# A GRU over 128 steps on one core: two more steps' inputs loaded ahead of r's last input weight, their reset products moved to the start, z's biases spread in another PSUM bank

## The chip, the cores and the metric

The kernel runs on one core of a Trainium2 chip. Its time is the device time of one execution in microseconds (us). The kernel before takes 1255.2 us, the median of three runs (1254.98 to 1255.48). A separate execution was profiled; durations below come from it.

## The reference

A batch of B = 64 sequences of T = 128 steps and width D = 512 goes through a GRU (gated recurrent unit) with state width 512, all in float32, and the result is added to the input:

```
for t in 0 .. 127:
    z = sigmoid([x_t, h] @ Wz + bz)          # Wz, Wr, Wh: 1024 x 512
    r = sigmoid([x_t, h] @ Wr + br)
    c = tanh([x_t, r * h] @ Wh + bh)
    h_new = (1 - z) * h + z * c
    h = tanh(h_new @ Wp + bp) if t % 4 == 3 and t < 127 else h_new
    out[:, t] = x_t + h_new
```

The first 512 rows of each weight meet x (here called the input weights, tile `wx`), the last 512 meet the state (`wh`). The input products do not depend on the state and may be computed ahead of the step that needs them; the state products may not.

## The kernel before, in words

The batch is cut into two halves of 32 (h = 0, 1) that run through the recurrence a little apart, so that one half's elementwise work lies under the other's products. A product of one step, one gate and one k (a quarter of the inner dimension, K = 4) is a *unit* (L246, called through `product` and `plain_unit`): four instructions of 128 x 32 by 128 x 256, eight records in the trace (each float32 product shows as two).

From group 2 on (a group is four steps) the input products are made by a scheme that shares products between steps. The first four steps, group 0, are done plainly: `plain(t, gates)` gives their units. Steps 0 and 1 are made ahead of the recurrence. Some units of steps 2 and 3 also stand ahead of it, the others are put in a queue from which the recurrence fills its gaps (`fill`, with the number of units per place in `HEAD`, `PLACES` and `TAIL`).

The order of the instructions on each engine is the order in which the Python code issues them (the pool is in manual schedule); only the waits are derived from what is read and written. What matters here is the start:

- **SP's DMA queue.** Rows of step 0 (L141; step 1's go through ACT's queue), r's input weight in three pieces (k = 0, k = 1, k = 2 and 3; `load_wx`, L127), z's and h's input weight in two pieces each, then step 2's x (`load_step(2)`, four transfers of 32 KB, L122), the state weight of r (L108), step 3's x (`load_step(3)`), the state weights of z and h, and the later loads. Each transfer of SP uses one of eight semaphores in turn, so it is issued when the transfer eight places before it (ACT's L141 among them) has landed. All of SP's transfers go to the same DMA queue.
- **GpSimd (POOL)** issues the biases' loads (L145), then copies one element of r's third piece (L154). Because of that copy it issues the initial state's rows (L156) only when the piece has landed. After VectorE's `sum_outer_1` it makes sums of weights.
- **TensorE (PE).** 28 products with zeros (`idle`), the transposes of steps 0 and 1 (`turn_rows`, L306), four more with zeros; r's units of steps 0 and 1 for k 0, for k 1, for k 2 and 3, as the pieces land; z's units of steps 0 and 1 in two halves, with the bias spreads between them; h's units of steps 0 and 1; then `both(8)`, eight units of step 2 (r and z); then step 0 of the recurrence, from `rec<-wh,hT_init`.
- **The biases.** `split_bias` (L205 to L210, VectorE) cuts them into three bfloat16 parts. `spread` (L217) multiplies these by a picking matrix into a PSUM bank, and ACT copies the result to `bias_x` (L226). r's and h's go to `scratch_y`, z's to the second half of `scratch_a`. `add_bias` (L483, VectorE) adds a bias to finished units and writes `cp`, from which ACT seeds the accumulators (`seed`, L442).
- **VectorE (DVE)** in order: copies of the turned rows (L311), `split_bias`, inner sums of input weights for r and z (L362 to L365, twice four), `add_bias` of r for steps 0 and 1, the first inner sum for h, `join_x(0, 2)` (L297, turns step 2's x into `xT`, the products' left side), the second inner sum for h, `sum_outer_1` (L354), the turn of the initial state (`hT_init`, L284), `add_bias` of z, `join_x(0, 3)`, `add_bias` of h and of step 2's r and z.

PSUM banks are named `scratch_q, r, a, x, y`. Step 0 has r in q's first half, step 1 in a's; step 2 has r in q's first and z in its second half, step 3 the same in a (`banks`). A unit that is first to write a bank is marked so (`start`); a gate that comes second in its bank is not marked (`second` in `plain_unit`).

Of the kernel before, what the change touches and what calls it, by code (L numbers as in the profile page):

```python
# [18 lines left out]
def kernel(  # L19
# [18 lines left out]
    S = 2  # L38
# [57 lines left out]
    def part(q):  # L96
        return slice(q * V, (q + 1) * V)
# [20 lines left out]
        xr[g] = xrp.tile([P, Q4, S, J], F32, tag="xr", name=f"xr_{g}")  # L118

    def load_step(t):  # L120
        for q in (0, 2, 1, 3):
            nc.sync.dma_start(  # L122
                out=xr[0][part(q), t], in_=x[:, t, ts(q, J)].rearrange("(h b) u -> b h u", h=S)
            )

    def load_wx(i, k0, k1):
        nc.sync.dma_start(  # L127
            out=wx[:, k0:k1, i, :],
            in_=gates_in[i][:D].rearrange("(p k) n -> p k n", k=K)[:, k0:k1],
        )  # L130
# [8 lines left out]
    )  # L139
    for t in range(2):  # L140
        both_queues[t].dma_start(out=x_rows[:, ts(t, D)], in_=x[:, t, :])  # L141
    for k0, k1 in ((0, 1), (1, 2), (2, K)):
        load_wx(R, k0, k1)
    for i, b in enumerate((br, bh, bz)):
        nc.gpsimd.dma_start(out=bias_in[:, i, :], in_=b.rearrange("(q j) -> q j", q=NQ))  # L145
    dummy = const.tile([1, 1], F32, name="dummy")
# [2 lines left out]
    for i in (Z, H_):  # L149
        for k in (0, 2):  # L150
            load_wx(i, k, k + 2)
    load_step(2)
    held = const.tile([1, 1], F32, name="held")
    nc.gpsimd.tensor_copy(held, wx[0:1, 3, R, 0:1])  # L154
    for h in range(S):
# [47 lines left out]
    def split_bias():  # L203
        high, low = thirds[:NQ], thirds[2 * V : 2 * V + NQ]
        nc.vector.tensor_copy(high, bias_in)  # L205
        nc.vector.tensor_sub(rest, bias_in, high)
        nc.vector.tensor_copy(middle, rest)
        nc.vector.tensor_copy(thirds[V : V + NQ], middle)
        nc.vector.tensor_sub(rest, rest, middle)
        nc.vector.tensor_copy(low, rest)  # L210
# [80 lines left out]
    def join_x(g, i):  # L291
        if g * Q4 >= T:
            return
        if g not in xT:
            xT[g] = xtp.tile([P, Q4, C, P], F32, tag="xT", name=f"xT_{g}")
        src = xr[g] if g < FIRST else xs[g]
        nc.vector.transpose(  # L297
            out=xT[g][:, i].rearrange("p c (a h b) -> p h (c a) b", a=S, h=S),
            in_=src[:, i].rearrange("p h (e k) -> p h k e", k=K),
        )  # L300
# [173 lines left out]
    def banks(t):  # L474
        first, second = scratch[:2] if t % 2 == 0 else scratch[2:4]
        if t < 2:
            return first[:, : S * J], second[:, : S * J], scratch[4][:, ts(t, S * J)]
        return first[:, : S * J], first[:, S * J :], second[:, : S * J]

    def add_bias(t, gates):  # L480
        new_cp(t // 2)
        for i in gates:
            nc.vector.tensor_add(  # L483
                G[t][:, :, :, i, :],
                banks(t)[i].rearrange("p (h c n) -> p c h n", h=S, c=C),
                bias_x[:, :, :, i, :],
            )

    def plain_unit(t, e, k, start, end=None, gates=()):
        g, i = divmod(t, Q4)  # L490
        bank = (q_bank, q_bank, r_bank) if t % 2 == 0 else (a_bank, a_bank, x_banks[0])
        second = H_ if t == 1 else None if t == 0 else Z
        return (
            lambda h: product(
                banks(t)[e], h, xT[g][:, i], wx[:, :, e, :], k, start and e != second
            ),
            S * J,
            {bank[e]},
            end,
            {bank[e] for e in gates},  # L500
        )

    def plain(t, gates=(R, Z, H_)):
        order = [(e, k) for e in gates for k in range(K)]
        if t == Q4 - 1:
            order = [(e, k) for k in range(K) for e in gates]
        return [
            plain_unit(
                t,
                e,  # L510
                k,
                k == 0,
                *((lambda: add_bias(t, gates), gates) if t > 1 and (e, k) == order[-1] else ()),
            )
            for e, k in order
        ]
# [254 lines left out]
    def both(n):  # L771
        for _ in range(n):
            for h in range(S):
                for _ in fill(1, h):
                    pass

    def now(units):
        put(units)
        both(len(units))

    first = {i: [plain(t, (i,)) for t in range(2)] for i in (R, Z, H_)}
    idle(28)
    turn_rows(0, scratch[4])
    turn_rows(1, scratch[3])
    split_bias()
    idle(4)
    for part_k in (slice(0, 1), slice(1, 2), slice(2, K)):
        for t in range(2):
            now(first[R][t][part_k])
    load_wh(R)  # L790
    load_step(3)
    load_wh(Z)
    load_wh(H_)
    later_loads()
    for t in range(2):
        now(first[Z][t][:2])
    spread(scratch[4], slice(0, 2), (R, H_))
    spread(scratch[2][:, S * J :], slice(2, 3), (Z,))
    for t in range(2):
        now(first[Z][t][2:])  # L800
    for i in (1, 2):
        sum_inner(i, nc.vector, slice(0, 2))
    for t in range(2):
# [1 line left out]
    for h in range(S):  # L805
        seed(R, 0, h)
    sum_inner(1, nc.vector, slice(2, 3))
    join_x(0, 2)
    sum_inner(2, nc.vector, slice(2, 3))
    sum_outer_1(nc.vector)  # L810
    hT = new_T("hT", "hT_init")
# [3 lines left out]
    for t in range(2):  # L815
        add_bias(t, (Z,))
    seed(Z, 0, 0)
    join_x(0, 3)
    for half_k in (slice(0, 2), slice(2, K)):
        for t in range(2):  # L820
            now(first[H_][t][half_k])
# [4 lines left out]
        sum_inner(i, nc.gpsimd)  # L826
    sum_outer(3)
    nc.gpsimd.tensor_sub(bias_d, bias_x[:, 1], bias0)
    put(plain(2, (R, Z)) + plain(3) + plain(2, (H_,)))
    both(8)  # L830

    state = {0: (h_init, hT)}

# [384 lines left out]
```

## Time and profile before

| | |
|---|---|
| median of the runs | 1255.2 us |
| profiled execution | 1255.74 us |
| its span, first to last instruction | 1253.6 us |
| TensorE granted clock | 1.000 |
| TensorE busy in 7.70 to 9.19 us | 0.21 us of 1.49 |
| TensorE busy in 9.19 to 33.5 us | all of it |
| DMA in 7.70 to 9.19 us | 363 GB/s, share 1.02 |
| start of the recurrence (first weight load of step 0) | 21.42 us |

Times in the trace are counted from the span's start. A row of the timeline has the start, the length of the whole group of instructions in us, the engine (PEld is TensorE's weight load, SPq the DMA-issuing queue of SP), the line, the operation, output <- input with its shape, and how many; in brackets stands the idle time before it and what ended that. A row of the waits has who waited for what, then the sum in us, the number of times and the longest. A row of DMA issues has how many, KB each and the us from issue to landing. A row of a DMA queue has its packets, MB, and the time that they took as a share of sixteen engines in the window.

### The profile page before, as it was taken

The page shows a single profiled execution, that of the slowest core. Times are in us where ns is not written, and L with a number is a line of the kernel's source. Part 1 is how long each engine was busy: PE and PEld are TensorE (multiplying, and loading weights), DVE is VectorE, ACT ScalarE, POOL GpSimd, SP SyncE. Part 2 cuts the span into 40 slices and gives each one's busy share as a digit, 9 for nine tenths or more (in the row PEclk, how much of TensorE's full clock was granted, in tenths as well). Part 3 has the DMA queues.
Part 4 walks back from the last instruction along what each step waited for, and adds up shares of the span by engine and source line. Part 5 has one row for each costly group of instructions (what it writes and reads, how often), then busy time and mean ns, then how long its engine had stood idle before and what let it go on. Part 6 is the DMA issues. An engine that isn't in the chain of part 4 may idle for free.

```text
span 1253.6 us, 61573 instructions
## 1 busy us (share of the span) xinstructions
PE 1246.9 (99%) x26384; PEld 1174.0 (94%) x26384; DVE 806.2 (64%) x2177; ACT 830.0 (66%) x2666; POOL 908.8 (72%) x1032
## 2 busy tenths in 40 slices
PE   9999999999999999999999999999999999999998
PEld 5899999999999999999999999999999999999987
DVE  5666666666666666666666666666666666666554
ACT  2566666766666676766666667666666666666664
POOL 4988777777876778767778677786777777777630
PEclk9999999999999999999999999999999999999999
DMA  8311212121111110221201211111111112111011
GB/s 257 83 31 42 53 37 53 36 54 39 35 53 49 41 49 24 53 53 37 54 24 49 53 41 50 36 43 47 53 38 39 49 39 53 39 52 27 12 39 35
DMA packets 112360, 61.14 MB, mean 49 GB/s; under 512 B 12844, under 2 KB 109368, under 8 KB 112088
## 3 DMA queue, kind: packets, MB, share of 16 engines
q1 hardware_dynamic: 111656, 56.90, 16.8%
q8 instruction: 208, 3.41, 1.2%
q14 instruction: 64, 0.52, 0.1%
q0 software_dynamic: 256, 0.14, 0.1%
q10 hardware_dynamic: 176, 0.16, 0.0%
HBM read 40.38 MB, written 16.78 MB: 46 GB/s over the span
## 4 chain that ended last, share of the span: by engine, by line
PE 99%; DMA 1%; SPq 0%; DVE 0%; issue 0%; ACT 0%
PE rec L246 44%; PE rec_z L246 16%; PE scratch_r L246 14%; PE scratch_q L246 11%; PE scratch_a L246 5%; PE scratch_y L246 4%; PE scratch_x L246 4%; DMA wx<-in_L_cond_Wr_dram 1%; PE scratch_a L541 0%; PE scratch_r L541 0%; PE scratch_q L541 0%; PE scratch_y L541 0%; PE scratch_x L541 0%; SPq L127 0%; SPq L141 0%
## 5 line engine op out<-in xcount | busy, mean ns | idle before, releaser
L246 PE MATMUL rec<-wh,rhT 128*32 128x256 f32 x4032 | 370.1, 379 | 0.0
L246 PE MATMUL rec<-wh,hT 128*32 128x256 f32 x3008 | 276.2, 379 | 0.0
L246 PE MATMUL rec_z<-wh,hT 128*32 128x256 f32 x3008 | 276.2, 379 | 0.0
L246 PEld LDWEIGHTS rec<-wh,rhT 128*32 128x32 f32 x4032 | 247.5, 110 | 16.7 <-ACT rec L442 0.3
L281 ACT ACTIVATE scratch_r<-rec 64x128 f32<-64x128 f32 x504 | 126.0, 250 | 129.9 <-PE rec L246 65.4
L442 ACT COPY rec<-cp 64x256 f32<-64x256 f32 x504 | 186.9, 371 | 19.4 <-DVE cp L483 0.2
L246 PEld LDWEIGHTS rec_z<-wh,hT 128*32 128x32 f32 x3008 | 190.5, 110 | 6.2
L246 PEld LDWEIGHTS rec<-wh,hT 128*32 128x32 f32 x3008 | 184.0, 110 | 11.2 <-ACT rec_z L442 0.4
L281 ACT ACTIVATE rec_z<-rec_z 64x128 f32<-64x128 f32 x488 | 122.0, 250 | 91.3 <-PE rec_z L246 79.7
L281 ACT ACTIVATE c<-rec 64x128 f32<-64x128 f32 x504 | 136.7, 271 | 61.5 <-PE rec L246 50.4
L968 POOL TENSOR_TENSOR xr<-xr,h 128x256 f32<-128x256 f32 x125 | 109.3, 874 | 85.8 <-DVE h L1138 71.9
L711 POOL TENSOR_TENSOR cp<-mb,mb 128x768 f32<-128x768 f32 x76 | 139.1, 1830 | 9.4 <-DVE mb L677 5.7
L711 POOL TENSOR_TENSOR mb<-mb,mb 128x768 f32<-128x768 f32 x58 | 106.3, 1832 | 45.8 <-DVE mb L677 45.8
L711 POOL TENSOR_TENSOR cp<-mb 128x768 f32<-128x768 f32 x46 | 84.3, 1832 | 56.8 <-ACT rec_z L442 55.4
L246 PE MATMUL scratch_r<-tw,s 128*32 128x192 f32 x928 | 120.9, 326 | 0.0
L650 ACT COPY cq<-scratch_q 128x384 f32<-128x384 f32 x212 | 102.1, 481 | 19.4 <-PE scratch_q L246 17.9
L667 DVE TENSOR_TENSOR cx<-scratch_r,cx 128x384 f32<-128x384 f32 x106 | 59.0, 557 | 84.5 <-PE scratch_r L246 69.0
L246 PE MATMUL scratch_q<-tt,s 128*32 128x192 f32 x928 | 103.6, 326 | 0.0
L1102 DVE SCALAR_TENSOR_TENSOR keep<-rec_z,h 128x256 f32<-128x256 f32 x91 | 38.6, 424 | 95.6 <-ACT rec_z L281 89.2
L673 DVE TENSOR_TENSOR mb<-scratch_q,cx 128x384 f32<-128x384 f32 x106 | 59.0, 557 | 62.5 <-ACT cq L650 62.5
L1081 DVE TENSOR_TENSOR rh<-scratch_r,h 128x128 f32<-128x128 f32 x188 | 54.8, 292 | 59.2 <-ACT scratch_r L281 59.2
L246 PE MATMUL rec<-wp,hT 128*32 128x256 f32 x992 | 91.4, 379 | 0.0
(250 smaller groups left out, 3899.9 us busy)
## 6 DMA issues: line engine op xcount, KB each, us to landing
out_dram<-xr SPq DMA_DIRECT2D x250, 64.0 KB, 1.8
xr<-in_x_dram SPq DMA_DIRECT2D x248, 64.0 KB, 2.1
xs<-in_x_dram SPq DMA_DIRECT2D x240, 64.0 KB, 2.1
wx<-in_L_cond_Wz_dram SPq DMA_DIRECT2D x2, 512.0 KB
wx<-in_L_cond_Wh_dram SPq DMA_DIRECT2D x2, 512.0 KB, 9.5
wh<-in_L_cond_Wr_dram SPq DMA_DIRECT2D x2, 512.0 KB
wh<-in_L_cond_Wz_dram SPq DMA_DIRECT2D x2, 512.0 KB, 5.5
wh<-in_L_cond_Wh_dram SPq DMA_DIRECT2D x2, 512.0 KB
```

Of the source, the lines that this page charges most:

```text
L246: nc.tensor.matmul(ps[part(2 * h + c)], lhsT=left, rhs=rhs(c), start=start, stop=True, skip_group_check=True,)
L281: nc.scalar.activation(o, v, func)
L442: nc.scalar.copy(gate_ps(i, h)[rows].rearrange("p d (c n) -> p d c n", c=C), G[t][rows, :, :, i, :].rearrange("p c d n -> p d c n"),)
L650: nc.scalar.copy(c[:, :nm], ps[:, :nm])
L667: nc.vector.tensor_add(T2[what][:, :nm], r_ps[:, :nm], T2[what][:, :nm])
L673: nc.vector.tensor_add(blocks(1, 1), runs(q_ps[:, :nm]), runs(T2[what][:, :nm]))
L711: nc.gpsimd.tensor_add(dst, a, b)
L968: nc.gpsimd.tensor_add(o, o, h_new.rearrange("p h (k e) -> p h e k", k=K))
L1081: nc.vector.tensor_mul(rh[:, h, :], r_, h_old[:, h, :])
L1102: nc.vector.scalar_tensor_tensor(out=kept[0], in0=kept[1], scalar=1.0, in1=kept[2], op0=ALU.subtract, op1=ALU.mult,)
```

## The change

- `load_step(t)` issues two transfers of 64 KB (one for each half of the batch, to 128 partitions) in place of four of 32 KB (one for each quarter of the partitions, both halves). Both use runs of 512 bytes.
- `load_step(2)` and `load_step(3)` stand between the second and the third piece of r's input weight.
- r's units of steps 2 and 3 for k 0 and 1 stand behind those of steps 0 and 1, and ahead of the units for k 2 and 3, which are now those of four steps. `both(8)` ahead of the recurrence is gone. The queue begins with z of step 2, z and h of step 3, h of step 2, sixteen units as before.
- VectorE turns steps 2 and 3 (`join_x`) ahead of `split_bias`. The adds of r's bias for steps 2 and 3 stand behind z's of steps 0 and 1.
- Steps 2 and 3 have r in the second half of their bank (q, a) and z in the first, so that r's units can run while the first half holds those of steps 0 and 1.
- z's biases are spread into the second half of `scratch_r` instead of `scratch_a`, after z's second half of units instead of ahead of it.

```diff
     def load_step(t):
-        for q in (0, 2, 1, 3):
+        for h in range(S):
             nc.sync.dma_start(
-                out=xr[0][part(q), t], in_=x[:, t, ts(q, J)].rearrange("(h b) u -> b h u", h=S)
+                out=xr[0][:, t, h], in_=x[ts(h, V), t, :].rearrange("b (q u) -> q b u", q=NQ)
             )
...
-    for k0, k1 in ((0, 1), (1, 2), (2, K)):
-        load_wx(R, k0, k1)
+    for k0 in range(2):
+        load_wx(R, k0, k0 + 1)
+    for t in (2, 3):
+        load_step(t)
+    load_wx(R, 2, K)
...
     for i in (Z, H_):
         for k in (0, 2):
             load_wx(i, k, k + 2)
-    load_step(2)
...
         if t < 2:
             return first[:, : S * J], second[:, : S * J], scratch[4][:, ts(t, S * J)]
+        if t < Q4:
+            return first[:, S * J :], first[:, : S * J], second[:, : S * J]
         return first[:, : S * J], first[:, S * J :], second[:, : S * J]
...
-        second = H_ if t == 1 else None if t == 0 else Z
+        second = (None, H_, R, R)[t] if t < Q4 else Z
...
-                *((lambda: add_bias(t, gates), gates) if t > 1 and (e, k) == order[-1] else ()),
+                *(
+                    (lambda: add_bias(t, gates), gates)
+                    if t > 1 and gates != (R,) and (e, k) == order[-1]
+                    else ()
+                ),
...
-    first = {i: [plain(t, (i,)) for t in range(2)] for i in (R, Z, H_)}
+    first = {i: [plain(t, (i,)) for t in range(Q4 if i == R else 2)] for i in (R, Z, H_)}
     idle(28)
     turn_rows(0, scratch[4])
     turn_rows(1, scratch[3])
-    split_bias()
     idle(4)
-    for part_k in (slice(0, 1), slice(1, 2), slice(2, K)):
-        for t in range(2):
-            now(first[R][t][part_k])
+    for ts_, parts in (
+        ((0, 1), (slice(0, 1), slice(1, 2))), ((2, 3), (slice(0, 2),)), (range(Q4), (slice(2, K),))
+    ):
+        if 2 in ts_ and 0 not in ts_:
+            join_x(0, 2)
+            join_x(0, 3)
+            split_bias()
+        for part_k in parts:
+            for t in ts_:
+                now(first[R][t][part_k])
     load_wh(R)
-    load_step(3)
     load_wh(Z)
...
     spread(scratch[4], slice(0, 2), (R, H_))
-    spread(scratch[2][:, S * J :], slice(2, 3), (Z,))
     for t in range(2):
         now(first[Z][t][2:])
+    spread(scratch[1][:, S * J :], slice(2, 3), (Z,))
...
-    join_x(0, 2)
...
     seed(Z, 0, 0)
-    join_x(0, 3)
+    for t in (2, 3):
+        add_bias(t, (R,))
...
-    put(plain(2, (R, Z)) + plain(3) + plain(2, (H_,)))
-    both(8)
+    put(plain(2, (Z,)) + plain(3, (Z, H_)) + plain(2, (H_,)))
```

## Prediction

> **What bounds the kernel now.** I read the page first (busy shares), then the waits of TensorE, then the timeline of the first 30 us, then the DMA answers. The page and the waits give:
>
> ```profile
> span 1253.6 us, 61573 instructions
> PE 1246.9 (99%) x26384; PEld 1174.0 (94%) x26384; DVE 806.2 (64%) x2177; ACT 830.0 (66%) x2666; POOL 908.8 (72%) x1032
> ```
>
> ```profile
> PE scratch_q L246 <- DMA wx<-in_L_cond_Wr_dram: 1.3, 1, 1.3
> PE rec L236 <- DVE zeros L67: 1.2, 1, 1.2
> ```
>
> TensorE (PE) is busy for all but 6.7 us. These are the two longest of its waits (a third row, for VectorE, is all that the list has beside them). The first is where this change is: the wait for the third piece of r's input weight, 1.3 us. Nothing else in 1250 us can be won, and the change leaves the number of products as it was: it moves some in the first 30 us. So the question is when TensorE starts step 0, and whether anything behind that is late. The weight-load rows (PEld) mark where each stretch starts, and DVE and ACT rows give the chain beside it:
>
> ```profile
> 5.98 0.64 PE L246 MATMUL scratch_q<-wx,xT 128*32 128x256 f32 x8 [0.17 <-DVE xT L311]
> ```
> ```profile
> 9.19 0.59 PEld L246 LDWEIGHTS scratch_q<-wx,xT 128*32 128x32 f32 x16 [1.76 <-DMA wx<-in_L_cond_Wr_dram]
> 9.87 0.78 PEld L246 LDWEIGHTS scratch_a<-wx,xT 128*32 128x32 f32 x16
> 10.73 0.78 PEld L246 LDWEIGHTS scratch_r<-wx,xT 128*32 128x32 f32 x16
> 11.59 0.78 PEld L246 LDWEIGHTS scratch_x<-wx,xT 128*32 128x32 f32 x16
> 12.46 0.55 PEld L217 LDWEIGHTS <-picks 96*32 96x32 bf16 x16
> 12.95 0.62 PEld L246 LDWEIGHTS scratch_r<-wx,xT 128*32 128x32 f32 x16
> 13.65 0.78 PEld L246 LDWEIGHTS scratch_x<-wx,xT 128*32 128x32 f32 x16
> 14.52 3.37 PEld L246 LDWEIGHTS scratch_y<-wx,xT 128*32 128x32 f32 x64
> 17.97 3.37 PEld L246 LDWEIGHTS scratch_q<-wx,xT 128*32 128x32 f32 x64
> 21.42 0.55 PEld L246 LDWEIGHTS rec<-wh,hT_init 128*32 128x32 f32 x6
> ```
> ```profile
> 7.22 0.35 DVE L205 CAST thirds<-tw 4x384 bf16<-4x384 f32 x1 [1.28 <-DMA tw<-in_L_cond_bz_dram]
> ...
> 9.41 0.35 DVE L210 CAST thirds<-tw 4x384 bf16<-4x384 f32 x1
> 10.62 0.42 DVE L362 TENSOR_TENSOR tt<-wx 128x256 f32<-128x256 f32 x1 [0.86 <-DMA wx<-in_L_cond_Wz_dram]
> ...
> 13.81 0.42 DVE L483 TENSOR_TENSOR cp<-scratch_q,bias_x 128x256 f32<-128x256 f32 x1
> ...
> 14.47 0.28 DVE L362 TENSOR_TENSOR tt<-wx 128x128 f32<-128x128 f32 x1
> ...
> 16.66 0.67 DVE L297 STREAM_TRANSPOSE xT<-xr 128x256 f32<-128x256 f32 x1 [1.06 <-DMA xr<-in_x_dram]
> 17.26 0.25 DVE L362 TENSOR_TENSOR tt<-wx 128x128 f32<-128x128 f32 x1
> ...
> 18.27 1.82 DVE L354 TENSOR_TENSOR d<-wx 128x768 f32<-128x768 f32 x2
> 20.01 0.50 DVE L284 STREAM_TRANSPOSE hT_init<-h_init 128x128 f32<-128x128 f32 x2
> ```
> ```profile
> 13.12 0.65 ACT L226 COPY bias_x<-scratch_y 128x256 f32<-128x256 f32 x2 [10.27 <-DVE tt L363]
> ```
>
> Read: products run without a break from 9.19 to step 0 at 21.42. A stretch of 64 records (eight units) takes 17.97 - 14.52 = 3.45 us, so a unit (one step, one k) takes 0.43. The four units of r's first two pieces end at 5.98 + 4 x 0.43 = 7.70; then TensorE waits till 9.19.
>
> **The change part by part.** *Products moved.* Steps 2 and 3 get their four units of r for k 0 and 1 (1.72 us) ahead of the third piece, and their four for k 2 and 3 right behind it. The eight units that stood ahead of step 0 (17.97 to 21.42) are gone from there. Let P be the moment at which everything for k 2 and 3 is at hand. From P to step 0 TensorE then has: eight units of r, 10.73 - 9.19 = 1.54 for the first four and 1.73 (12.46 - 10.73, the same four with no wait ahead) for the others; four of z, 1.73; the two bias spreads and four of z, 14.52 - 12.46 = 2.06; h's eight, 3.45. Together 10.51.
>
> *The loads.* What was first hidden behind all input weights now stands in SP's queue ahead of r's third piece: four transfers of 64 KB in 512-byte runs, in a form that SP elsewhere issues only for the last-but-one output step (L998, DRAM side 4 x 32 x 128):
>
> ```profile
> 2.26 1.01 SPq L127 DMA_DIRECT2D wx<-in_L_cond_Wr_dram  x2
> ```
> ```profile
> wx<-in_L_cond_Wr_dram SPq DMA_DIRECT2D x1, 256.0 KB, 4.2
> ```
> ```profile
> 1246.08 1.30 SPq L998 DMA_DIRECT2D out_dram<-xr  x2
> ```
> ```profile
> q1 hardware_dynamic: 173, 0.09, 28.6%
> ```
> ```profile
> q1 hardware_dynamic: 1463, 0.66, 44.1%
> ```
> ```profile
> q1 hardware_dynamic: 198, 0.38, 102.3%
> ```
>
> The fourth fence is the DMA answer for 1248 to 1249, when only the two stores of that form run: 28.6% of sixteen engines, that is 4.6 of 16, and 173 packets in a microsecond. Stores of this form do not spread over sixteen engines; I read it as four, a little overlapped. The fifth is 27 to 33 us, when only loads of 512-byte runs move: 0.441 x 6 x 16 us / 1463 = 28.9 ns of one engine for a packet. The sixth is 11 to 12 us under weights alone: 198 packets per us, so a 512 KB piece (256 packets) takes 1.29 us. The four new loads hold 4 x 128 packets; on four engines that is 128 each, 128 x 28.9 ns = 3.70 us, on sixteen 0.92. I take 3.70.
>
> The Trainium skill, "DMA: Bandwidth & Descriptors", section "Why a DMA increments its semaphore by 16 and not by 1", has the rule: a transfer runs on the largest number of engines up to sixteen that divides the slowest dimension of both sides. The old loads have 32 there on both sides, the new ones 4 on the DRAM side. It speaks against this change, and the trace's 4.6 of 16 agrees with it.
>
> The second piece lands at 2.26 + 4.2 = 6.46. Behind it step 2's rows land at 6.46 + 1.85 = 8.31, step 3's at 10.16, and the third piece, behind them on the same four engines, at 11.45. VectorE's transpose of a step is 0.67, and it stands idle there (its bias split is put behind the transposes). So step 2's two units start at 8.31 + 0.73 = 9.04 (0.06 for the hand-over, an estimate) and step 3's at 10.16 + 0.73 = 10.89, ending at 11.75. P = 11.75, a little later than the third piece. The wait of 9.19 - 7.70 = 1.49 us becomes two, 1.34 and 10.89 - 9.90 = 0.99.
>
> *What is late next.* Without the eight units ahead of step 0 its state hT is the next thing awaited. The spread of r's and h's biases starts at P + 5.00; ACT copies it 0.66 later (12.46 to 13.12), the first copy takes 0.33, so VectorE's add of r starts at P + 6.05. Then: adds 14.47 - 13.81 = 0.66, two inner sums of 18.27 - 17.26 = 1.01, the outer sum 20.01 - 18.27 = 1.74, the first half's turn 0.25: hT at P + 10.72. TensorE is there at P + 10.51 and waits some 0.27 with the hand-over. VectorE reaches that add in time: the split from 10.83 for 9.76 - 7.22 = 2.54, then the eight sums of 13.81 - 10.62 = 3.19, done at 16.6 against P + 6.05 = 17.8 (their weights, z's two pieces, land at 12.7 and 14.0 by the pace above). The change also makes z's first filler of step 2 wait for the add of r's bias for step 2 (order of the built program), three adds (1.05) behind the second turn; TensorE has twelve products first, about 1.3 us: nothing, and 0.2 at most.
>
> *The rest.* z's spread in another bank and four bias rows less in the fillers are the same instructions at another place: nothing. Later weights: six pieces of 1.29 behind 11.45 put r's state weight at 19.2, needed at P + 10.5 = 22.3. GpSimd (POOL) waits for the third piece before it issues h's rows, and for the outer sum before its own sums:
>
> ```profile
> 9.20 0.22 POOL L154 COPY held<-wx 1x1 f32<-1x1 f32 x1 [5.97 <-DMA wx<-in_L_cond_Wr_dram]
> 9.37 1.43 POOL L156 DMA_DIRECT2D tw<-in_cond_dram  x2
> ```
> ```profile
> tw<-in_cond_dram POOLq DMA_DIRECT2D x2, 64.0 KB, 6.3
> ```
>
> With the third piece at 11.45 the second half of h's rows is issued at 12.4 and lands at 18.7, needed (behind ACT's copies) by about 21. POOL's sums start some 2 us later against TensorE's 1.2. No row of TensorE's list of waits names POOL; I cost it at nothing.
>
> **Sum.** Step 0 starts at P + 10.51 + 0.27 = 22.5 instead of 21.42: about +1.1 us, of which the narrow loads are all and more; I take +1.2 with a little for the small waits. The profiled execution took 1255.74 (2.1 us around its span of 1253.6), so 1256.9 there; the median of the runs is 0.5 below it, 1255.2, so 1256.4.
>
> **The rivals.**
> *Sixteen engines.* Were loads spread where stores are not, step 3's rows land at 7.38, its units end at 9.42 in the old wait, and the third piece is 0.92 later: P = 10.11, step 0 at 20.9, -0.5 us: 1254.7. Against it: the 4.6 of 16.
> *The packets are dear (slower).* Place: the four engines between 6 and 12 us, with weights streaming on the other twelve. Early weights paid more than later ones:
>
> ```profile
> q1 hardware_dynamic: 103, 0.19, 85.5%
> ```
>
> This is 3.5 to 4.5 us: 0.855 x 16 us / 103 = 133 ns a packet against 1.023 x 16 / 198 = 83 at 11 us, 1.6 times. At 1.6 x 28.9 = 46 ns the rows of step 3 land at 12.4, P = 13.95, +3.3 us with the rest as above: 1258.5. It decides (over 0.2%, 2.5 us) from about 40 ns a packet. For it: nothing shows this form loading in a busy queue; against: by 11 us the dear stretch is over.
> *h or VectorE late.* If h's rows pay the same 1.6 (10 us to land) they come at 22.4 and step 0 stands 0.8 longer: 1257.2.
> *The gap is simply filled:* rows early and the third piece not late, 1.3 us off: 1253.9.
>
> **How the numbers follow.** Forecast 0.55 (1256.4, its own range 1255.7 to 1257.5), sixteen engines 0.13, dear packets 0.20, late h 0.08, filled 0.04. A measurement of this kernel tells about 0.2% (2.5 us) from no change; a gain that large isn't there to be had, as TensorE waits 1.3 us in all for what is moved, so faster gets 0.01. Slower gets the dear packets and a little of late h on top, 0.23, same 0.76. The range takes in sixteen engines below and dear packets above: 1254.6 to 1258.6.
>
> **What would show it.** The four loads at some 0.3 of sixteen engines, step 3's rows landing 1.8 us behind step 2's; two waits of TensorE for VectorE's xT of about 1.3 and 1.0 in place of that for Wr; a short wait for hT; step 0 at 22.5. Wrong, if the rows land before 8 us, if TensorE waits for Wr again, or if step 0 stands over 0.5 us for something not named here.

## The result and the profile after

The changed kernel takes 1257.86 us, the median of 22 runs (1257.28 to 1259.59); the kernel before takes 1255.54 on the same chip (22 runs, 1254.84 to 1256.76). The ratio is 1.002, with a 95% interval of 1.0013 to 1.0026: 1.6 to 3.3 us more. The forecast was +1.2. The difference of the medians, 2.3 us, stays just under the 2.5 us (0.2%) from which the prediction would have called a change one. The profiled execution took 1257.88.

The first two lines of the page of the changed kernel, and, from the list of TensorE's weight-load waits, the rows for VectorE's xT (they stand in place of the wait for Wr), for hT and for POOL:

```profile
span 1255.8 us, 61567 instructions
PE 1249.5 (100%) x26384; PEld 1170.6 (93%) x26384; DVE 806.8 (64%) x2177; ACT 830.6 (66%) x2666; POOL 909.3 (72%) x1032
```
```profile
PEld scratch_a L248 <- DVE xT L299: 0.7, 1, 0.7
PEld rec L248 <- DVE hT_init L286: 0.5, 1, 0.5
PEld scratch_y L248 <- POOL s L377: 0.4, 1, 0.4
PEld scratch_q L248 <- DVE xT L299: 0.3, 1, 0.3
```

No row of TensorE names Wr any more. Two rows were not forecast at this size: hT for 0.5, and POOL's sums for 0.4. The first two units on the timeline of TensorE's products, then three rows of its weight loads, after:

```profile
5.92 1.07 PE L248 MATMUL scratch_q<-wx,xT 128*32 128x256 f32 x8
6.78 1.07 PE L248 MATMUL scratch_a<-wx,xT 128*32 128x256 f32 x8
```
```profile
10.88 0.59 PEld L248 LDWEIGHTS scratch_a<-wx,xT 128*32 128x32 f32 x16 [0.74 <-DVE xT L299]
11.56 0.78 PEld L248 LDWEIGHTS scratch_q<-wx,xT 128*32 128x32 f32 x16
22.68 1.48 PEld L248 LDWEIGHTS rec<-wh,hT_init 128*32 128x32 f32 x28 [0.51 <-DVE hT_init L286]
```

VectorE's turns of steps 2 and 3, the first add of r's bias, the turn of hT, and the last operation:

```profile
8.33 0.64 DVE L299 STREAM_TRANSPOSE xT<-xr 128x256 f32<-128x256 f32 x1 [2.27 <-DMA xr<-in_x_dram]
10.18 0.65 DVE L299 STREAM_TRANSPOSE xT<-xr 128x256 f32<-128x256 f32 x1 [1.22 <-DMA xr<-in_x_dram]
...
17.80 0.42 DVE L487 TENSOR_TENSOR cp<-scratch_q,bias_x 128x256 f32<-128x256 f32 x1 [1.07 <-ACT bias_x L228]
...
22.32 0.50 DVE L286 STREAM_TRANSPOSE hT_init<-h_init 128x128 f32<-128x128 f32 x2
...
1251.70 0.29 DVE L1064 TENSOR_TENSOR xr<-z,xr 128x128 f32<-128x128 f32 x1
```

The first two units start 6.78 - 5.92 = 0.86 us apart: in this execution a unit takes twice the 0.43 of the kernel before. And the DMA queue of the loads from 6 to 6.5 us:

```profile
q1 hardware_dynamic: 82, 0.04, 28.4%
```

Read: the two turns start 10.18 - 8.33 = 1.85 us apart, and the bus is at 28.4% of sixteen engines, so the narrow loads behave as forecast. (From 7.5 us on, when weights move beside them, the share is 96% and more.) The units for k 2 and 3 start at 11.56 and step 0 at 22.68, against 21.42. POOL's copy of one element of the third piece, which waits for that piece, starts at 11.29 (9.20 before), and its sums at 22.54 (20.23 before):

```profile
11.29 0.40 POOL L156 COPY held<-wx 1x1 f32<-1x1 f32 x1 [8.07 <-DMA wx<-in_L_cond_Wr_dram]
...
22.54 0.17 POOL L837 COPY held<-d 1x1 f32<-1x1 f32 x1 [9.43 <-DVE d L356]
```

The end, in both kernels. First the kernel before: its last VectorE operation, then how many GB/s were moved in forty slices of 0.275 us from 1251 us on; then the same slices after:

```profile
1250.20 0.29 DVE L1052 TENSOR_TENSOR xr<-z,xr 128x128 f32<-128x128 f32 x1
```
```profile
GB/s 60 63 56 108 11 30 0 0 0 0 0 0 0 0 0 0 0 0 0 0 0 0 0 0 0 0 0 0 0 0 0 0 0 0 0 0 0 0 0 0
```
```profile
GB/s 52 8 60 17 43 47 13 120 15 105 0 0 0 0 0 30 0 0 0 0 0 0 0 0 0 0 0 0 0 0 0 0 0 0 0 0 0 0 0 0
```

Before, the output's last packets stand in the fifth slice, and the 30 in the sixth is one packet of the queue that brings instructions. After, the output ends in the tenth slice and that packet comes in the sixteenth, six slices or some 1.6 us later. VectorE ends 1.50 us later, and the span (1253.64 and 1255.78 in the packed traces) 2.14: **0.6 us come after the last operation**. From the end of the last output packet to the span's end there is a gap of 1.45 us before and 2.07 after. The packet of instructions is not what is waited for: after, it starts at 1255.36, when SyncE's last wait for the output has been over for 0.5 us. What the gap is made of stands below, at the end of the span.

The 2.1 us by place: the first row of h of step 0 comes 33.33 - 32.26 = 1.07 later (below); at 110 us another 0.2 is added (from 1.09 to 1.28), at TensorE's wait for POOL; 0.1 that comes little by little up to 1060 us and 0.1 in the last steps are unnamed; the end adds 0.6. The lag between the two traces was read from VectorE's and ACT's rows, matched one by one. Two rows of h, of before and of after, and the weight load that waits for POOL:

```profile
32.26 0.29 DVE L1138 TENSOR_TENSOR h<-rec_z,keep 128x128 f32<-128x128 f32 x1
```
```profile
33.33 0.29 DVE L1150 TENSOR_TENSOR h<-rec_z,keep 128x128 f32<-128x128 f32 x1
```
```profile
110.13 0.11 PEld L248 LDWEIGHTS scratch_y<-tt,s 128*32 128x32 f32 x2 [0.35 <-POOL s L377]
```

### The profile page after: what moved, and what is told of

Its sections match the earlier page's. It is cut to its first block, busy times and chain, and to the rows that moved or that the text cites. A ratio compares the mean times of both kernels' runs of the same rounds, so it can differ in the third digit from the quotient of the medians.

```text
span 1255.8 us, 61567 instructions
## 1 busy us (share of the span) xinstructions
PE 1249.5 (100%) x26384; PEld 1170.6 (93%) x26384; DVE 806.8 (64%) x2177; ACT 830.6 (66%) x2666; POOL 909.3 (72%) x1032
## 4 chain that ended last, share of the span: by engine, by line
PE 99%; DMA 0%; SPq 0%; DVE 0%; issue 0%; ACT 0%; DVEq 0%
PE rec L248 44%; PE rec_z L248 16%; PE scratch_r L248 14%; PE scratch_q L248 10%; PE scratch_a L248 5%; PE scratch_y L248 4%; PE scratch_x L248 4%; PE scratch_a L549 0%; PE scratch_r L549 0%; DMA xr<-in_x_dram 0%; PE scratch_q L549 0%; PE scratch_y L549 0%; SPq L122 0%; PE scratch_x L549 0%; SPq L127 0%; DVE xT L299 0%
```

## The experiments

The theory was that the narrow loads hold the third piece of Wr, and all that follows it, back. Its rivals were that the place itself costs (bytes on a full bus, or issues ahead of the piece), that VectorE's order costs (hT, POOL), or that something else does at the end.

**The old form at the new place.** `load_step` of the kernel before in the changed one (the transfer in the loop goes with it):

```
-        for h in range(S):                              # 2 x 64 KB, 4 x 32 x 128
+        for q in (0, 2, 1, 3):                          # 4 x 32 KB, 32 x 2 x 128
...
```

> The changed kernel with the old form of the x loads (four of 32 KB a step, 32 x 2 x 128 on both sides) at the new place. Narrow-load theory: step 2's and 3's rows no longer crawl on four engines; DMA share over the loads well above 0.5 instead of 0.28, step 3's first product clearly ahead of the changed kernel's 10.88 us (about 8.5 to 9.5). But eight issues of about 0.42 us, the last ones behind the landing of the second piece (6.46) and the third piece behind that of step 2's first load, put the third piece at about 11 to 11.5, so that step 0 starts at about 22 to 22.3, against 22.68, and the time is 0 to 0.6 us under the changed kernel's. Cover rival (the chain to hT sets step 0, whenever the loads land): step 0 at 22.5 to 22.7, no change.

1256.31 (10 runs; ratio to before 1.0005, 0.9996 to 1.0014). Its weight loads:

```profile
8.05 0.59 PEld L248 LDWEIGHTS scratch_q<-wx,xT 128*32 128x32 f32 x16 [0.44 <-DVE xT L299]
8.93 0.59 PEld L248 LDWEIGHTS scratch_a<-wx,xT 128*32 128x32 f32 x16 [0.29 <-DVE xT L299]
10.87 0.59 PEld L248 LDWEIGHTS scratch_q<-wx,xT 128*32 128x32 f32 x16 [1.34 <-DMA wx<-in_L_cond_Wr_dram]
...
21.80 1.48 PEld L248 LDWEIGHTS rec<-wh,hT_init 128*32 128x32 f32 x28 [0.51 <-DVE hT_init L286]
```

The rows of the two steps are 0.88 apart instead of 1.85: the form sets the rate. But TensorE waits for Wr again, 1.34 us, now behind eight units instead of four: SP's eight issues take 3.89 us, and the third piece is issued at 6.67 (5.24 with the narrow form). From 6.5 to 7.5 us the bus is at 30% and 13% only, so here it is the issues and not the bytes that keep the piece back. The wait that was to be filled is still there. The time is 1.55 us below the changed kernel's, where 0 to 0.6 was expected: 0.9 of it is step 0 (21.80 against 22.68), and the gap at the end of the span is 0.7 shorter (below).

```profile
2.74 3.89 SPq L122 DMA_DIRECT2D xr<-in_x_dram  x8
...
6.67 0.44 SPq L127 DMA_DIRECT2D wx<-in_L_cond_Wr_dram  x1
```

**The narrow form at the old place.** The kernel before with the new `load_step` alone.

> The kernel before with the new form of the x loads (two of 64 KB a step, DRAM side 4 x 32 x 128) at the old places. Narrow-load theory: step 2's rows take 64 packets on each of four engines, so VectorE's transpose starts about 1 us later than 16.66 and TensorE waits 0.3 to 1 us ahead of step 2's units (17.97); the time is 0.3 to 1 us over the kernel before. Rival (the form spreads over sixteen engines like the old): the transpose at 16.7 or earlier, since there are two issues less, and no change.

1257.05 (10 runs; 1.0008, 0.9999 to 1.0017). Step 2's rows are turned 0.7 us later than before and step 3's 1.1 later, and TensorE does not wait for either; in the second execution of the kernel before (below) they are later still, at 17.88 and 22.29 against 17.35 and 22.18 here. Step 0 stands at 22.05, 0.63 late, but its units took 0.85 us until about 10.4 in this execution, and the third piece came at 9.40. The time can't be put down to how the rows arrive; 0.5 to 0.6 of the 0.96 us over the kernel before stand at the end of the span, which has the changed kernel's long gap (1.95).

**The turn of hT first.** VectorE turns hT ahead of h's sums and the outer sum:

```
-    sum_inner(1, ...); sum_inner(2, ...); sum_outer_1(nc.vector)
     ...                        # the turn of h_init stands here
+    sum_inner(1, ...); sum_inner(2, ...); sum_outer_1(nc.vector)
```

> The changed kernel with the turn of the initial state ahead of h's inner sums and the outer sum on VectorE. If the chain to hT is worth the 0.51 us that TensorE waited ahead of step 0, that wait goes, step 0 starts at about 22.2 and the time is 0.5 us lower than the changed kernel's; no other part of its loss goes. If the wait only moves (the outer sum late for GpSimd, adds late for the seeds), step 0 starts earlier and the end does not: 0 to 0.2 us.

1262.04 (5 runs; 1.0046, 1.0033 to 1.006; the profiled execution is the fastest of the five, 1260.59). Step 0 starts at 22.20 with no wait, and then this stands first in the weight loads' waits:

```profile
PEld scratch_q L248 <- DVE cp L487: 2.4, 1, 2.4
```

z's filler of step 2 waits for the add of r's bias for step 2. That add stands behind the sums as in the changed kernel, but VectorE first waits for the copy of the initial state, which is not there before 20.7, and all behind it is late:

```profile
20.70 0.65 DVE L286 STREAM_TRANSPOSE hT_init<-h_init 128x128 f32<-128x128 f32 x2 [2.20 <-ACT h_init L822]
```

POOL's wait grows to 0.9. The edge that the prediction held for 0.2 at most is worth 2.4 us as soon as that add moves back by 2.4 (it is VectorE's row at 23.38 in the changed kernel, 25.76 here): it had little slack. In the changed kernel the add ends at 23.79 and the filler starts at 24.22, which leaves some 0.4 us.

**The third piece in two.** The kernel before with k 2 and k 3 loaded and used apart.

> The kernel before with r's third input weight piece loaded as two of 256 KB (k 2, k 3), its products ordered by k. If the 1.5 us wait ahead of k 2 can be had by smaller pieces alone: k 2 lands at about 8.2 to 8.6, its two units (0.86 us) lie in the wait for k 3 (about 9.2 to 9.5), step 0 starts 0.5 to 0.9 us earlier than 21.42, and the time falls by 0.5 to 0.9 us where TensorE is at full speed. Clock rival: where TensorE's first units take 0.85 us each as in the changed kernel's profile, they end at about 9.3 and there is no wait to fill: no change.

1256.63 (11 runs; 1.0006, 0.9997 to 1.0015). Weight loads:

```profile
7.54 0.24 PEld L246 LDWEIGHTS scratch_q<-wx,xT 128*32 128x32 f32 x8 [0.19 <-DMA wx<-in_L_cond_Wr_dram]
...
9.78 0.16 PEld L246 LDWEIGHTS scratch_q<-wx,xT 128*32 128x32 f32 x8 [1.57 <-DMA wx<-in_L_cond_Wr_dram]
...
11.10 0.59 PEld L246 LDWEIGHTS scratch_r<-wx,xT 128*32 128x32 f32 x16 [0.73 <-DMA wx<-in_L_cond_Wz_dram]
```

The wait only moves to k 3 and to z, and step 0 stands at 21.61, not 0.5 to 0.9 earlier. I read it so: in this stretch the stream of weights paces TensorE, and bytes put ahead of it must be paid.

**VectorE's sums while it waits anyway.** The changed kernel with h's sums, the outer sum and the turn of hT ahead of the adds of r's bias, in the 1.07 us for which VectorE waits for the spread.

> The changed kernel with one part of VectorE's order turned: h's inner sums, the outer sum and the turn of hT stand ahead of the adds of r's bias for steps 0 and 1 and r's seeds, so that they fill the 1.07 us for which VectorE waits for the spread of r's bias. The reset layer's order and all loads stay. Theory (the wait of 0.51 us for hT ahead of step 0 and the wait of 0.4 us for POOL's s at 64 us are both VectorE's late start of h's sums, and each carries through to the end): step 0's weight load begins at 22.1 to 22.2 instead of 22.68 with no wait for hT, POOL's first sum some 1.8 us earlier than 22.5, its wait in the list of TensorE's waits gone, and the time 0.5 to 0.9 us below the changed kernel's: 1257.0 to 1257.4 where that runs 1257.9. Rival (another wait only takes their place: z's fillers wait for the add of r's bias, as they did with the sums ahead of all adds): a wait of scratch_q for cp of 0.5 us or more stands in the list, and the time is the changed kernel's or above it.

1257.77 (11 runs; 1.0017, 1.0008 to 1.0026); the changed kernel in the same rounds took 1257.96. The trace does what it should: no wait for hT, and POOL's falls from 0.35 to 0.19, which the kernel before has too in one of its two executions (its place is 110 us; the 64 us of the expectations was misread).

```profile
12.01 0.59 PEld L248 LDWEIGHTS scratch_q<-wx,xT 128*32 128x32 f32 x16 [0.80 <-DMA wx<-in_L_cond_Wr_dram]
...
22.52 1.66 PEld L248 LDWEIGHTS rec<-wh,hT_init 128*32 128x32 f32 x28
```

From 12.01 to 22.52 are 10.51 us, the products alone; in the changed kernel it is 22.68 - 11.56 = 11.12. But the first four units of r take 12.68 - 12.01 plus 0.86, since they follow a wait, and 2 x 0.86 in the changed kernel, where none stands ahead. With nothing ahead and no wait for hT the stretch is 22.20 - 11.50 = 10.70 in the run with the turn first. So the order is worth 0.4 us at step 0, and at most 0.2 at POOL. The time shows 0.2 of the 0.5 to 0.9 expected, within the spread. In the profiled execution the third piece came 0.7 later than in the changed kernel's (12.02), and a weight load in the last step had to wait 0.35 us for its own issue.

**Rows of 4 KB.** Steps 2 and 3 as one load of 64 rows, turned by TensorE, copied by VectorE (`x_rows_2` is a second buffer, and the later load of group 0's x takes all four steps); then the same with the order above.

```
-    for t in (2, 3): load_step(t)
+    nc.sync.dma_start(out=x_rows_2, in_=x[:, 2:4, :].rearrange("b t d -> b (t d)"))
...
-            join_x(0, 2); join_x(0, 3)
+            turn_rows(2, scratch[4]); turn_rows(3, scratch[3])
```

> The changed kernel with x of steps 2 and 3 loaded at the same new place, but as one transfer of 64 rows of 4 KB, like steps 0 and 1, and turned by TensorE and copied out by VectorE in place of the four narrow loads and VectorE's joins. Theory (all that the new place costs is the narrow form's low rate, which keeps the third piece of the input weight from the bus until 11.2): the third piece lands at about 10, the last ld of r's products begins at 9.9 to 10.4, step 0 at 20.7 to 21.1, and the time is 1.6 to 1.9 us below the changed kernel's and 0.3 to 0.7 us below that of the kernel before. Where the granted clock of the first units is low until 9 us or later, the four extra turns and products eat 0.3 to 0.6 of that. Rival (any load between the two pieces costs its bytes on a bus that is full, and the turns cost TensorE what the joins cost VectorE): step 0 at 21.4 or later and the time within 0.3 us of the kernel before.

> The two together: rows of steps 2 and 3 as one transfer of 4 KB rows, and h's sums and the turn of hT ahead of r's adds. If the causes add up: step 0 at 20.4 to 20.8 with no wait for hT, no wait for POOL's s at 64 us, and the time 0.5 to 1.2 us below the kernel before. If VectorE becomes what the reset layer waits for (its copies of the turned rows, then the sums, then the adds that z's fillers need): a wait of scratch_q for cp of 0.4 us or more, and the time that of the run with the rows alone, or above it.

1256.70 and 1256.44 (11 runs each; 1.0008, 0.9999 to 1.0017, and 1.0006, 0.9997 to 1.0015). With the rows alone:

```profile
6.94 0.16 PEld L250 LDWEIGHTS scratch_q<-wx,xT 128*32 128x32 f32 x8 [0.47 <-DMA wx<-in_L_cond_Wr_dram]
...
8.24 0.55 PEld L310 LDWEIGHTS scratch_y<-ident,x_rows 64*128 64x128 f32 x4 [0.71 <-DMA x_rows<-in_x_dram]
...
9.45 0.59 PEld L250 LDWEIGHTS scratch_q<-wx,xT 128*32 128x32 f32 x16 [0.17 <-DVE xT L315]
...
22.11 1.48 PEld L250 LDWEIGHTS rec<-wh,hT_init 128*32 128x32 f32 x28 [0.51 <-DVE hT_init L288]
```

About half of the loss is back (1.3 and 1.5 us against the changed kernel in the same rounds; the gap at the end of the span is 0.3 to 0.6 shorter), but not the gain that I expected over the kernel before: step 0 was to be at 20.7 to 21.1. The third piece is no longer waited for; instead TensorE waits 0.47 for the second and 0.71 for the rows, and the turns take 8.24 to 9.45. The rival holds in the trace (1.49 us of waiting have become 1.18 of waiting and 1.2 of turning), though not in its time: that is 1.3 and 1.1 above the median of the kernel before in these rounds, not within 0.3. With the order of the sums step 0 is at 22.08, without hT's wait, from rows that came 0.4 later.

**Issues on two queues.** The old form, step 2's four issues on SP, step 3's on ACT's queue, and the order above.

> The changed kernel with three edits drawn from the runs so far: x of steps 2 and 3 in the kernel before's small wide pieces (32 KB, all sixteen engines), step 2's four issued by SyncE and step 3's four by ScalarE's queue, which is idle from 2.9 us on, so that the third piece of r's input weight is issued at about 4.7 instead of 5.24 or, with eight on SyncE, 6.67; and h's sums and the turn of hT ahead of r's adds. Theory (the place costs nothing but the rate of the narrow form, the issue time of many small pieces on one queue, and VectorE's order): the rows are joined by 8.2, the third piece lands at 9.6 to 10.0, step 0 begins at 20.3 to 20.8 without a wait for hT, and the time is 0.3 to 1.0 us below the kernel before. Rival (the bytes themselves: 256 KB more ahead of the third piece on a full bus, so that TensorE's wait for it only moves, and what step 0 gains is lost again at z's fillers, whose adds now stand behind the sums): step 0 at 21.2 or later, or a wait of scratch_q for cp of 0.4 us or more, and the time within 0.3 us of the kernel before or above it.

1256.75 (11 runs; 1.0005, 0.9996 to 1.0014). Step 0 at 22.11, which is the rival's number, by a cause that neither named: TensorE waits for no load at all, but its units take 0.85 us until 10.4, so there was no wait to be won in this execution. Nor did the edit do what it was made for: SP's issues for step 2 start at 3.58 (2.74 in the others), the third piece is issued at 6.19 and not at about 4.7, the rows are turned by 9.1 and not by 8.2, and the piece is there at 10.69 and not at 9.6 to 10.0. It leaves the theory untested.

```profile
3.58 2.56 SPq L122 DMA_DIRECT2D xr<-in_x_dram  x4
6.19 0.43 SPq L127 DMA_DIRECT2D wx<-in_L_cond_Wr_dram  x1
```
```profile
8.06 0.23 PEld L248 LDWEIGHTS scratch_a<-wx,xT 128*32 128x32 f32 x4 [0.20 <-issue]
8.48 0.23 PEld L248 LDWEIGHTS scratch_a<-wx,xT 128*32 128x32 f32 x4 [0.20 <-issue]
...
10.19 0.22 PEld L248 LDWEIGHTS scratch_q<-wx,xT 128*32 128x32 f32 x4 [0.20 <-issue]
10.55 0.78 PEld L248 LDWEIGHTS scratch_a<-wx,xT 128*32 128x32 f32 x16
```

**Both kernels once more.**

> The changed kernel once more, on the chip and in the rounds of the three others, as their yardstick: 1257.3 to 1258.2, some 1.5 to 2.5 us above the kernel before. Its profile tells whether two things stay with the kernel or go with the execution: the granted clock of TensorE's first units (0.85 us a unit until 9.8 in the first profile) and the 0.7 us by which the span's end stood later behind VectorE's last operation. Theory: the joins, the third piece and step 0 come at the same times within 0.1 us (11.56 and 22.68), since the loads set them, and the end behind VectorE's last operation is anywhere from 3.4 to 4.1. Rival: it is again 4.1, and belongs to the kernel.

> The kernel before, profiled a second time, in the rounds of the three others. Theory: the gap from its last output packet to the end is again 1.3 to 1.6 us, and the time 1255.0 to 1256.0. Rival: the gap goes with the execution, and is anything from 1.3 to 2.2. Its profile also tells whether the third piece's landing (a wait of 1.49 us that ends the products' gap) moves from one execution to the next as the changed kernel's did, by 0.2 to 0.4 us, and from which time on TensorE's units take 0.43 us.

1257.96 (11 runs; 1.0016, 1.0008 to 1.0025) and 1255.29 (11 runs; 0.9995, 0.9986 to 1.0004). The weight loads of the changed kernel, then of the kernel before:

```profile
9.00 0.59 PEld L248 LDWEIGHTS scratch_q<-wx,xT 128*32 128x32 f32 x16 [1.60 <-DVE xT L299]
11.09 0.59 PEld L248 LDWEIGHTS scratch_a<-wx,xT 128*32 128x32 f32 x16 [1.50 <-DVE xT L299]
11.76 0.78 PEld L248 LDWEIGHTS scratch_q<-wx,xT 128*32 128x32 f32 x16
...
22.89 1.48 PEld L248 LDWEIGHTS rec<-wh,hT_init 128*32 128x32 f32 x28 [0.51 <-DVE hT_init L286]
```
```profile
9.77 0.64 PEld L246 LDWEIGHTS scratch_q<-wx,xT 128*32 128x32 f32 x16 [1.11 <-DMA wx<-in_L_cond_Wr_dram]
...
22.06 1.66 PEld L246 LDWEIGHTS rec<-wh,hT_init 128*32 128x32 f32 x28
```

The start moves from one execution to the next: step 0 of the kernel before at 21.42 and 22.06, of the changed kernel's lead-in at 22.68, 22.89, and in the two runs that follow 22.29 and 21.81. Means 21.74 and 22.42: 0.7 us apart, where the two first profiles gave 1.26. These means are rough: the second execution of the kernel before is the slowest of its eleven runs (1256.92, median 1255.29), and that with sixteen more issues the fastest of its eleven (1256.65, median 1257.80). My limit of 0.1 us for this was too narrow. The gap at the end stayed: 1.94 and 1.33.

The moment at which POOL's copy shows the third piece landed tells place and form apart:

| what stands ahead of the third piece | third piece there at, us |
|---|---|
| nothing: before (twice), narrow at the old place | 9.20, 9.78, 9.41 |
| narrow loads: after (twice), turn first, sums first, five more, sixteen more | 11.29, 11.48, 11.26, 12.02, 10.90, 10.72 |
| old form; two queues | 10.88; 10.69 |
| rows; rows and sums | 10.93; 10.03 |

The means are 9.5, 11.3 and 10.6 (the last two lines together). So of the 1.8 us by which the piece comes later some 1.2 go with the place, in whatever form, and the narrow form adds some 0.7. By these few executions, which scatter by up to 1.3 us, the theory names the smaller part.

**The end of the span.** The changed kernel with five, and then with sixteen, more issues on SP's queue in the middle of the run:

```
-            load_x(xr[g + 1], (g + 1) * Q4, Q4)
+            # group 5: five of the eight pieces as two halves (sixteen: groups 5 and 7, all eight)
+            load_x_parts(xr[g + 1], (g + 1) * Q4, Q4, 5 if g == 4 else 0)
```

> The changed kernel with five more DMA issues on SyncE's queue in the middle of the run (five of the eight 64 KB pieces of x of one later group as two pieces of 32 KB each), and nothing else. It looks at the end of the span: from the last packet of the output to the span's end the kernel before and the two runs with its eight small loads took 1.3 to 1.5 us, five runs with the four narrow loads, which give SyncE four issues fewer, took 1.9 to 2.2, and the two with one load of rows 1.6 to 1.7; in that gap stands one packet of the queue that brings instructions. Theory (where that last packet falls goes by the number of instructions in SyncE's stream, not by the place or the form of the loads): with the count back near that of the kernel before, the gap is 1.3 to 1.6, the packet comes within 0.5 us of the last output packet, and the time is 0.5 to 0.7 us below the changed kernel's: 1257.2 where that is 1257.9. Rival (the gap belongs to the narrow loads or to the execution): it is 1.9 to 2.2 and the time that of the changed kernel.

> The same with sixteen more issues on SyncE's queue (two later groups, all eight pieces in two each). By the theory that the count sets the end, the gap from the last output packet to the end differs from the changed kernel's 2.1 in a way that stays from run to run; its size is not known ahead, between 1.3 and 2.2. By the rival it is 1.9 to 2.2 again.

With five more: 1257.18 (11 runs; 1.0010, 1.0001 to 1.0019), 0.7 below the changed kernel's medians (in other rounds, and with intervals that overlap), as expected. The first line of its page and the slices from 1251 us on:

```profile
span 1255.0 us, 61574 instructions
```
```profile
GB/s 2 0 49 11 60 19 101 63 56 60 0 30 0 0 0 0 0 0 0 0 0 0 0 0 0 0 0 0 0 0 0 0 0 0 0 0 0 0 0 0
```

The gap is 1.27. With sixteen more: 1257.80 (11 runs; 1.0015, 1.0007 to 1.0024), gap 1.69; the profiled execution is the fastest of the eleven, and the median does not show the 0.3 to 0.4 that the gap is shorter.

What the gap is made of can be read in the packed traces, which hold the semaphore instructions that the timeline leaves out. SyncE ends the program with eight waits, always in the same order, one for each of the eight semaphores that the transfers take in turn. From its last wait on, the rest takes 0.9 us in every execution. (Ahead of the gap, from VectorE's last operation to the output's last packet, 2.0 to 2.8 us pass, which differs by execution.) Two things differ. *The place of the last semaphore:* each wait that still follows the one for the output's last transfer adds 0.07. Four issues fewer move that transfer from the seventh semaphore to the third, so five waits follow instead of one. *A pause:* SyncE's 976th instruction starts at least 0.33 us after the one before it, in all fourteen executions. With four instructions fewer ahead of them, it is the sixth of the eight waits instead of the second: behind the last landing, no longer beside it. Together 4 x 0.07 + 0.3, the 0.6 us.

| executions | place of the last transfer's semaphore | SyncE's 976th instruction | gap, us |
|---|---|---|---|
| before (twice), old form | 7th | 2nd wait, output still landing | 1.3 to 1.5 |
| third in two, five more | 8th | 1st wait, output still landing | 1.3 |
| two queues | 7th | 6th wait, output still landing | 1.5 |
| rows, rows and sums | 8th | 8th wait, as the output lands | 1.5, 1.6 |
| sixteen more | 3rd | ahead of the output's last transfers | 1.7 |
| after (twice), narrow at the old place, turn first, sums first | 3rd | 6th wait, output landed | 1.9 to 2.1 |

The run with sixteen more (twice eight) keeps the third place and moves the pause away: some 0.3 over the kernel before are left. Five more give the eighth place. So the gap goes with the program's issues, wherever they stand. The packet of instructions does not matter: with sixteen more the next one starts after the span's end.

## Why the prediction was right, point by point

- **The narrow loads** were right: 64 packets at 28.9 ns are 1.85 us, and the turns stand 1.85 apart in the first profile, 1.69 to 2.08 in six executions (26 to 33 ns a packet); the share was to be some 0.3 and is 0.284. The packets were not dear beside the weights (that rival needed 40 ns), and not on sixteen engines. The rule of the Trainium skill that was cited ("DMA: Bandwidth & Descriptors", section "Why a DMA increments its semaphore by 16 and not by 1") gives these loads four engines of sixteen, and 28.4% agrees with it; with the slow dimension back at 32 the distance is about half (0.88).
- **P** was to be 11.75. In four executions of this lead-in it was 11.56, 11.76, 11.16 and 10.71. The forecast ends step 3's two units 0.86 after their start; they take 0.68, since they follow a wait. The two waits of 1.34 and 0.99 were 0.3 and 0.7 in the first profile, since units of 0.85 filled part of the time, and 1.6 and 1.5 in the second, with units of 0.43: P is set by the loads, as argued.
- **From P to step 0** the products take 10.70 and not 10.51: the sum took 1.54 for r's first four units, as behind a wait, but here they follow step 3's units without one. So the same 0.19 us is too much in P and too little behind it, and the two errors cancel (11.56 + 10.70 and 11.75 + 10.51 are both 22.26). The wait for hT was to be 0.27; it delays step 0 by 22.68 - 22.26 = 0.42 (the row's 0.51 has in it the short gap that stands between groups anyway). With it step 0 stood 11.10 to 11.13 behind P in all four.
- **POOL** was cost at nothing. That step failed: it started 2.3 us later, TensorE waited 0.4, and 0.2 stayed. In the four executions of this lead-in the wait is 0.29 to 0.38, with the sums first 0.19, and before 0.20 or none.
- **z's filler behind r's add**: nothing, as forecast, but with a margin of only 0.4 us (2.4 us of waiting in the run with the turn first).
- **Sum.** +1.2 forecast, +2.3 measured in the medians. The missing term is for the most part none of the start's: 0.6 us behind the last operation, which the prediction did not look at. With five more issues, which take that out, the kernel stands 1.4 us above the kernel before by the median of those rounds (1255.81) and 1.9 above the eleven runs that took it up again beside it (1255.29); of that, POOL is 0.1 to 0.2. So the forecast's +1.2 for the start is about there, and the runs can't tell it closer. The measured 1257.86 lies outside the forecast's own range (up to 1257.5). It lies within the whole range by luck, as that was drawn wide for packets that would be dear, and they were not.
- **The gain that was to be had** is small whichever way these loads went: whatever stood ahead of the third piece brought it 0.6 to 2.6 us later, where the wait was 1.49. In the small old form that goes with the issues (above). With the rows, one issue, it can be the bytes: 256 KB at the 363 GB/s of the full bus are 0.7 us by estimate, and the piece came 1.5 and 0.6 later than the mean before. Why one and the same queue lands it at moments over a microsecond apart stays open. Four versions of the new place without the narrow form came within 0.1% of the kernel before, none ahead of it.

## What to carry to other kernels

Before filling a wait for a load with work that needs another load, look at the DMA share in that stretch: if it is full, the new bytes push the awaited ones back. Count the issues ahead of the awaited load too (eight took 3.89 us here), and weigh them against the form: that with half the issues ran on about four engines of sixteen and took twice as long from step to step (1.85 against 0.88). Then follow every chain that loses its slack (here hT, POOL's sums, one add), not only the engine whose wait is removed. For differences of 0.1% take the lead-in from several executions, and look at the span's end by itself: there the number of DMA issues alone, anywhere in the program, was worth up to 0.8 us.

## What the runs showed of the hardware

- The time at which TensorE's units go from 0.85 to 0.43 us differs by execution, even of one kernel: in the kernel before it is ahead of 6.0 in one profile and behind 8.8 in the other, in the changed one 9.8 and 6.2; 10.4 with the narrow form at the old place and on two queues. The granted clock of the profile stands at 1.00 all the while. The Trainium skill, "TensorE: Matmul & The Clock Gate", section "What's actually happening", has a window of 3.4 us that runs freely and doesn't start with the kernel, and a transition that varies by 0.5 us. That it doesn't start with the kernel fits; the spread here is over 4 us, far more than 0.5.
- SyncE pauses at least 0.33 us ahead of its 976th instruction in all fourteen executions, and so it does ahead of its 80th, 208th, 336th, 464th, 592nd, 720th and 848th: every 128 instructions. The trace does not say for what. Where such a pause falls behind the last landing it lengthens the span.
- The last 1.3 to 2.1 us of a span, behind the output's last packet, depend on the number of DMA issues by this pause and by the place of the last transfer's semaphore in the closing row of waits (0.07 each): five more small issues in the middle of the run moved it by 0.8 us.
- With the same queue of loads P came between 10.71 and 12.01, from execution to execution.
